# One ring of eight PSUM banks, and the scores of two batches next to each other on TensorE

## The chip, the core and the metric

One core of a Trainium2 chip runs the whole program. The metric is the time of one execution on the device in microseconds (us). PE is TensorE, which multiplies matrices; DVE is VectorE, ACT ScalarE, POOL GpSimd, and SP is SyncE, which issues most of the transfers (DMAs). PSUM is the memory into which TensorE writes: 8 banks of 2 KB per partition.

## What is computed

128 batches of 128 tokens with 512 features go through two graph layers, in float32:

```python
h = maximum(layernorm(x), 0)                        # layer 0
q, k, v = h @ Wq.T + bq, h @ Wk.T + bk, h @ Wv.T + bv   # 8 heads of 64
attn = softmax((q @ k.T) * SCALE * (adj + adj))     # per batch and head, 128 x 128
x = x + (attn @ v) @ Wo.T + bo
h = maximum(layernorm(x), 0)                        # layer 1
Wh = h @ W;  e = leaky_relu(Wh @ a[:512] + (Wh @ a[512:]).T)
att = softmax(where(adj > 0.5, e, -9e15), axis=1)
x = x + elu(att @ Wh)
```

## The kernel before

Work goes by pairs of batches (p = 0 to 63; batches a and b of a pair), and q, k and v are made for groups of two pairs. Everything is written as short named steps, and three lists of step names give the order: HEAD once, ORDER once per loop pass (57 passes), TAIL once. In HEAD and TAIL `step@p` names the pair (in TAIL counted from the end), in ORDER `step:lag` works on the pair that many passes back. A step that a pair does not have is skipped. The order on every engine and every queue is the order of these lists; nothing reorders it, and the tile pools only add the waits.

The steps that matter here, with the lines of their functions:

- `U1` to `U11` (L230 `product`): one of the 21 partial products of q, k, v, four matmuls 128x256 into a PSUM tile acc_a, acc_b or acc_c. `F` steps copy a finished tile out on ScalarE (L262, L267), `A` steps add one on VectorE (L271). Products of the same tile follow each other into the same bank.
- `sca`, `scb` (L302 `scores`): scores of batch a or b, eight matmuls that use 64 rows of the array each (one head each; heads on rows 0 to 63 and on rows 64 to 127 alternate). `ata`, `atb` (L315 `weigh`): VectorE multiplies the scores by the adjacency out of PSUM into the tile `at`. `mxa` (L323) takes the maxima, `exa0` to `exa3` (L327) the exponentials on ScalarE, `rca0/1` and `nma0` to `nma3` (L332, L336) normalise, `fla` (L343) flips 32x32 blocks on VectorE, `bla` and `pla` (L348, L352) send the blocks to DRAM and fetch them placed, one DMA and four, all on SyncE's queue.
- `pca`, `pcb` (L367 `context`): the context of a batch, eight matmuls of 64 columns each, into a tile pc; `pea` (L382) copies it out on ScalarE. `cs0` to `cs3` (L146 to L152) are sums on VectorE.
- `o0` to `o6` and `w0` to `w6` (L283 `product_rows`): the products with Wo and with W, two matmuls each into row_a or row_c; `od`, `wd` (L389, L471) add on VectorE and `zc` (L467) copies on ScalarE. `wd1` adds what `w1` made to what `zc0` copied. `gs0` to `gs3` are VectorE sums for W.
- `st0/1`, `pw`, `nm`, `h20/1`, `d..`, `pb`, `wm`, `g0/1`, `ge0/1`: layer 1, with `pw` on GpSimd and `pb`, `g` on TensorE.
- In the head, `lx`, `Lq`, `Lk`, ... load x and the weights on SyncE's queue; `Wq0` and the like (L132 `weight_sum`) are VectorE sums over a weight that has landed; `t0`, `t1` (L172) are row statistics, `pp` the power on GpSimd, `hn` (L178) normalises, `tp` (L186) transposes on TensorE, `ev` (L191) copies out on ScalarE.

PSUM is divided in two pools: `ps1`, six single banks that all other tiles take in turn, and `ps2`, one tile of two banks, only for scores. Scores of heads on rows 0 to 63 go into the first of the two banks, the others into the second.

In ORDER these steps stand as `sca:0 pca:1 pcb:1 scb:0` as far as TensorE is concerned: between them are steps of other engines only. So a loop pass has scores of batch a, two contexts of the pair before, and scores of batch b.

Of the kernel before, what the change touches and what calls it, by code (L numbers as in the profile page):

```python
# [13 lines left out]
P = 128  # L14
# [10 lines left out]
def kernel(  # L25
# [31 lines left out]
    ps1 = ctx.enter_context(tc.tile_pool(name="ps1", bufs=6, space=bass.MemoryType.PSUM))  # L57
    ps2 = ctx.enter_context(tc.tile_pool(name="ps2", bufs=1, space=bass.MemoryType.PSUM))
# [243 lines left out]
    def scores(b):  # L302
        p, i = divmod(b, 2)
        g, h = divmod(p, 2)
        qT, kT = qks[g, "q"][h], qks[g, "k"][h]
        cols = slice(i * S, (i + 1) * S)

        sc = ps2.tile([P, H, S], F32, name="sc", tag="ps2")
        for j in range(C):
            for s in range(2):  # L310
                r = slice(s * D, (s + 1) * D)
                nc.tensor.matmul(sc[:, s * C + j, :], qT[r, j, cols], kT[r, j, cols], start=True, stop=True)  # L312
        scs[b] = sc

    def weigh(b):  # L315
        p, i = divmod(b, 2)
        at = work.tile([P, H, S], F32, name="at")
        nc.vector.scalar_tensor_tensor(  # L318
            at, scs.pop(b), QSCALE, adjs[p][:, i : i + 1, :].to_broadcast([P, H, S]), op0=OP.mult, op1=OP.mult
        )  # L320
        ats[b] = at, small.tile([P, H], F32, name="nmx"), small.tile([P, H], F32, name="sums"), small.tile([P, H], F32, name="rs")
# [210 lines left out]
    def listed(text, mark):  # L532
# [3 lines left out]
        lx@0 t0@-5 Lu0@0 t1@-5 lt@0 Lq@0 Lk@0 pp@0 lx@1 hn0@0 hn1@0 tp0@0 Wq0@0 Lu1@0 t1@-4 t0@-4 tp1@0 pp@1 Wq2@0 hn0@1  # L536
        ev0@0 Lv@0 ev1@0 U3@-1 U5@-1 Wk0@0 U1@-2 lx@2 hn1@1 F1@-2 tp1@1 Lo@0 tp0@1 Wq1@0 la@-1 Lw@0 ev0@1 la@0 ev1@1
        t1@-3 t0@-3 U8@-2 U6@-2 F3@-1 pp@2 l0@-2 U2@-2 hs0@-3 F6@-2 l0@-1 hs1@-3 Wk1@0 U10@-2 Wv0@0 Lc@0 Wk2@0 Wk3@0
        hn0@2 hs2@-3 U7@-1 F7@-1 Wv1@0 A5@-1 hs3@-3 t0@-2 U3@-2 F10@-2 t1@-2 pp@3 A8@-2 hn1@3 tp0@2 U2@-1 U9@-1 hn0@3
        hn1@2 F3@-2 cu01@0 F2@-1 U4@-1 F9@-1 tp1@2 cu00@0 U8@-1 l0@0 ev0@2 ev1@2 A9@-1 U10@-1 tp0@3 Ww0@0 l0@1 t0@-1  # L540
        U11@-1 U5@-2 F4@-1 t1@-1 F10@-1 sca@0 F5@-2 tp1@3 ata@0 mxa@0 exa2@0 exa3@0 exa0@0 ccp@0 A2@-2 Wv2@0 ccd@0 U1@0
        ev0@3 t1@0 sh@0 ev1@3 rca1@0 U6@0 U7@-2 nma2@0 Wq3@0 t0@0 F6@0 hs0@-1 cu10@0 s0@-1 nma3@0 exa1@0 U1@-1 rca0@0
        lt@1 scb@0 hs1@-1 F7@-2 U3@1 nma0@0 nma1@0 A2@-1 fla@0 atb@0 U10@0 mxb@0 U6@-1 exb0@0 Wv3@0 U4@-2 t1@1 bla@0
        U2@0 exb2@0 A11@-1 exb1@0 rcb0@0 exb3@0 t0@1 nmb0@0 A5@-2 f0@0 rcb1@0 nmb1@0 nmb3@0 pla@0 s0@0 A6@-1 Wo0@0 U9@-2
        sup0@0 hs2@-1 nmb2@0 sca@1 Wo2@0 f0@1 flb@0 sua0@0 ata@1 blb@0 A9@-2 lT@1 F10@0 U8@0 F3@1 U2@1 A8@0 F1@0 mxa@1
        plb@0 la@1 cu11@0 hs3@-1 exa2@1 exa0@1 U3@0 F2@1 exa1@1 rca0@1 exa3@1 nma1@1 U5@1 U4@1 U7@1 A2@0 nma0@1 Wo1@0
        Ww2@0 rca1@1 scb@1 F4@1 Ww1@0 nma3@1 nma2@1 lT@0 F7@1 l0@2 pca@0 F3@0 A5@1 fla@1 pcb@0 pea@0 sup1@0 U9@1 atb@1
        mxb@1 peb@0 exb2@1 U8@1 U5@0 sua1@0 cs0@0 bla@1 s0@1 Ww3@0 hd0@0 pla@1 hd1@0 exb1@1 o0@0 f0@2 o1@0 F9@1 hd0@1
        hd1@1 exb3@1 exb0@1 U10@1 od0@0 F10@1 cs1@0 od1@0 rcb1@1 nmb3@1 U1@1 rcb0@1 nmb2@1 F5@0 o2@0 nmb1@1 A9@1 sca@2
        hs0@1 nmb0@1 A2@1 pca@1 U6@1 od2@0 Wo3@0 cs2@0 o4@0 flb@1 o3@0 ata@2 cs3@0 od4@0 U11@1 od4c@0 blb@1 o5@0 mxa@2  # L550
        o6@0 exa3@2 exa2@2 od5@0 hs2@1 exa0@2 exa1@2 U4@0 t1@2 rca1@2 nma3@2 hs1@1 A5@0 A6@1 od6@0 rca0@2 nma2@2 st0@0
        U7@0 pea@1 nma0@2 U1@2 A11@1 st1@0 o0@1 plb@1 nma1@2 F7@0 pcb@1 scb@2 sh@1 fla@2 pw@0 peb@1 atb@2 U2@2 o1@1
        mxb@2 F1@2 bla@2 nm@0 U3@2 h21@0 exb2@2 cs0@1 cs1@1 U4@2 U9@0 h20@0 A2@2 d11@0 od0@1 exb3@2 d00@0 od1@1 hs3@1
        d10@0 F3@2 o2@1 lT@2 d01@0 od2@1 exb0@2 rcb1@2 pb@0 exb1@2 U5@2 wm@0 rcb0@2 pr@0 F5@2 nmb1@2 cs2@1 U6@2 m1@0
        o4@1 e1@0 t0@2 lt@2 U7@2 nmb0@2 cs3@1 nmb3@2 A5@2 A9@0 pla@2 sw@0 F7@2 od4@1 o3@1 g0@0 nmb2@2 o5@1 ge0@0 od4c@1
    """
    ORDER = """
        F4:1 F6:1 flb:1 fb:4 U9:1 F9:1 g1:3 od5:2 ge1:3 o6:2 la:1 st0:2 s0:1 hd0:1 od6:2 U8:1 w0:3 st1:2 gs0:3 blb:1
        hd1:1 pw:2 w1:3 gs1:3 nm:2 U10:1 zc0:3 so:4 U1:0 gs2:3 h20:2 A9:1 A8:1 l0:0 wd1:3 w2:3 F10:1 gs3:3 h21:2 plb:1
        lx:1 hs0:1 zc2:3 lT:0 sca:0 pca:1 pcb:1 scb:0 w4:3 d00:2 d01:2 pea:1 A6:1 ata:0 mxa:0 peb:1 d10:2 w3:3 F1:0  # L560
        d11:2 cs0:1 t1:0 exa1:0 f0:0 exa3:0 pb:2 sh:1 A4:4 wm:2 zc4:3 exa2:0 exa0:0 pr:2 o0:1 o1:1 rca1:0 F8:0 nma3:0
        hs2:1 w5:3 hs1:1 wd4c:3 rca0:0 U2:0 nma1:0 cs2:1 cs1:1 nma2:0 m1:2 nma0:0 w6:3 od0:1 U11:1 od1:1 fla:0 U3:0
        zc5:3 atb:0 F2:0 mxb:0 F3:0 o2:1 e1:2 A10:16 cs3:1 wd6:3 U5:0 F5:0 sw:2 exb0:0 A2:0 U4:0 exb2:0 A3:28 exb3:0
        exb1:0 A5:0 A11:1 bla:0 o3:1 rcb1:0 od2:1 nmb2:0 U6:0 hs3:1 o4:1 lt:0 rcb0:0 nmb0:0 t0:0 nmb3:0 nmb1:0 pla:0
        U7:0 ez:3 F7:0 F11:-22 g0:2 fa:3 od4:1 A1:15 od4c:1 ge0:2 o5:1 A7:14
    """
    TAIL = """
        F4@-5 U9@-5 F9@-5 g1@-7 flb@-5 o6@-6 A6@-5 U10@-5 fb@-8 la@-5 ge1@-7 gs0@-7 F10@-5 so@-8 hd0@-5 od5@-6 blb@-5
        pca@-5 sca@-4 hd1@-5 pea@-5 la@-4 U5@-3 st0@-6 lx@-5 U8@-5 ata@-4 mxa@-4 exa0@-4 exa3@-4 exa1@-4 od6@-6 w0@-7
        hs0@-5 w1@-7 o0@-5 scb@-4 exa2@-4 st1@-6 pw@-6 U3@-3 gs2@-7 A9@-5 zc0@-7 nm@-6 rca0@-4 rca1@-4 hs1@-5 wd1@-7  # L570
        nma3@-4 nma0@-4 gs1@-7 nma2@-4 o1@-5 gs3@-7 plb@-5 sh@-5 nma1@-4 fla@-4 pcb@-5 atb@-4 U11@-5 od0@-5 U6@-4 F3@-3
        h21@-6 peb@-5 h20@-6 mxb@-4 exb0@-4 w2@-7 d10@-6 cs0@-5 exb3@-4 exb2@-4 zc2@-7 U7@-3 cs1@-5 A11@-5 d00@-6
        exb1@-4 od1@-5 w4@-7 F6@-4 d11@-6 o2@-5 pb@-6 rcb0@-4 od2@-5 rcb1@-4 wm@-6 nmb1@-4 d01@-6 nmb0@-4 sca@-3 w3@-7
        nmb2@-4 U10@-4 nmb3@-4 zc4@-7 w5@-7 cs2@-5 bla@-4 scb@-3 pr@-6 flb@-4 ata@-3 cs3@-5 hs2@-5 zc5@-7 pla@-4 m1@-6
        wd4c@-7 pca@-4 mxa@-3 w6@-7 F7@-3 o4@-5 od4@-5 wd6@-7 F10@-4 e1@-6 U2@-3 blb@-4 exa1@-3 exa0@-3 sw@-6 plb@-4
        fa@-7 exa2@-3 o5@-5 ez@-7 pea@-4 rca0@-3 g1@-6 nma0@-3 exa3@-3 o3@-5 la@-3 od5@-5 U9@-3 st0@-5 rca1@-3 od4c@-5
        g0@-6 o6@-5 ge1@-6 fb@-7 gs0@-6 o0@-4 A5@-3 nma2@-3 nma3@-3 pcb@-4 ge0@-6 nma1@-3 gs1@-6 w0@-6 o1@-4 fla@-3
        atb@-3 so@-7 lx@-4 mxb@-3 F9@-3 od6@-5 w1@-6 F2@-3 peb@-4 hs3@-5 cs0@-4 zc0@-6 wd1@-6 st1@-5 U8@-4 U10@-3 pw@-5
        bla@-3 exb3@-3 exb2@-3 exb1@-3 w2@-6 gs2@-6 gs3@-6 pla@-3 nm@-5 cs1@-4 exb0@-3 cs2@-4 rcb1@-3 la@-2 h21@-5
        rcb0@-3 zc2@-6 nmb3@-3 A8@-4 U8@-3 nmb2@-3 sh@-4 nmb0@-3 nmb1@-3 F10@-3 w4@-6 od0@-4 d11@-5 cs3@-4 od1@-4 zc4@-6  # L580
        d10@-5 U4@-3 F4@-3 U1@-3 sca@-2 flb@-3 w3@-6 h20@-5 ata@-2 o3@-4 mxa@-2 w5@-6 wd4c@-6 zc5@-6 d00@-5 exa0@-2
        o2@-4 od2@-4 w6@-6 o4@-4 A2@-3 d01@-5 wd6@-6 exa3@-2 od4@-4 lt@-4 exa1@-2 fa@-6 exa2@-2 pca@-3 ez@-6 U6@-3 pb@-5
        fb@-6 rca0@-2 blb@-3 o5@-4 od4c@-4 wm@-5 nma0@-2 rca1@-2 pr@-5 od5@-4 nma3@-2 A6@-3 o6@-4 plb@-3 nma1@-2 U1@-4
        U2@-4 nma2@-2 pcb@-3 m1@-5 scb@-2 st0@-4 pea@-3 od6@-4 st1@-4 fla@-2 e1@-5 A9@-3 so@-6 sw@-5 peb@-3 o0@-3 g1@-5
        g0@-5 U11@-3 ge1@-5 pw@-4 atb@-2 lx@-3 o1@-3 F1@-4 ge0@-5 cs0@-3 nm@-4 mxb@-2 cs2@-3 h21@-4 exb1@-2 gs0@-5 o3@-3
        w0@-5 sh@-3 lt@-3 w1@-5 exb0@-2 exb3@-2 h20@-4 gs1@-5 od0@-3 A11@-3 U3@-4 exb2@-2 A2@-4 rcb0@-2 d10@-4 cs1@-3
        zc0@-5 nmb0@-2 od1@-3 d00@-4 rcb1@-2 cs3@-3 o2@-3 d01@-4 wd1@-5 nmb1@-2 od2@-3 nmb2@-2 nmb3@-2 gs2@-5 sca@-1
# [46 lines left out]
    def steps(p):  # L634

        table = start_steps(p)
        for s, n in (("a", 2 * p), ("b", 2 * p + 1)):
            table |= {
                "sc" + s: lambda n=n: scores(n),
                "at" + s: lambda n=n: weigh(n),  # L640
                "mx" + s: lambda n=n: maxima(n),
                "fl" + s: lambda n=n: flip_blocks(n),
                "bl" + s: lambda n=n: send_blocks(n),
# [121 lines left out]
```

## Time and profile before

| what | value |
| --- | --- |
| median of 3 runs | 2380.54 us (2380.22 to 2381.16) |
| the profiled execution, its own time | 2378.95 us |
| its span, first to last instruction | 2377.1 us |
| granted TensorE clock | 1.000 |
| ScalarE busy | 1457.4 us (61%) |
| DMA | 306.10 MB, mean 129 GB/s |

The page of the profile gives busy time per engine, and the chain of work that ended last, followed back from the last instruction to what released each step. Groups of instructions are listed by line, engine and operation with the tiles that they write and read: `at<-sc,adj` is the tile `at` made from `sc` and `adj`; x128 is the count, then busy us and mean ns of one, then the idle time of the engine just before. A float32 matmul of the program is two records in the trace (1024 score matmuls are 2048 records). The modelled durations of matmuls overlap, so lengths on TensorE are taken between starts.

### The profile page before, as it was taken

Reading aid. Unit: us, or ns where it says so; the run is one execution under the profiler, and the core shown is the slowest. Engines: PE = TensorE matmul, PEld = TensorE weight load, DVE = VectorE, ACT = ScalarE, POOL = GpSimd, SP = SyncE. Lnnn points to the kernel's source line nnn. Section 1 sums busy time; section 2 is a strip of 40 time slices with the busy share of each in tenths; the row PEclk is TensorE's granted clock in tenths of the full one; section 3 lists DMA queues with packets and bytes.
Section 4 is the critical chain, followed back from the end, with each engine's and each line's share of the span. In section 5 each row is a group of like instructions: output and inputs, shape, how many; then the busy total and the mean of one; then the engine's idle time right before and its main releaser. Section 6 shows DMA issues by size and latency. Waiting matters only on the chain.

```text
span 2377.1 us, 40536 instructions
## 1 busy us (share of the span) xinstructions
PE 2355.3 (99%) x14264; PEld 2062.0 (87%) x14264; DVE 1988.5 (84%) x3909; ACT 1457.4 (61%) x4811; POOL 265.7 (11%) x323
## 2 busy tenths in 40 slices
PE   8999999999999999999999999999999999999998
PEld 7888888888888888888888888888888888888886
DVE  6878888888888888888888888888888888888787
ACT  3656566665666665656656666556656566665764
POOL 1011110111101101111111011111110111111000
PEclk9999999999999999999999999999999999999999
DMA  4444544554534545445455455453454544544332
GB/s 173 123 129 116 138 130 121 137 133 129 142 111 126 154 121 138 111 118 158 116 138 133 118 137 137 128 145 107 125 160 116 138 111 123 153 120 125 108 113 93
DMA packets 255275, 306.10 MB, mean 129 GB/s; under 512 B 21856, under 2 KB 181600, under 8 KB 254432
## 3 DMA queue, kind: packets, MB, share of 16 engines
q1 hardware_dynamic: 251568, 303.37, 46.5%
q8 instruction: 113, 1.85, 0.3%
q0 software_dynamic: 1920, 0.13, 0.2%
q14 instruction: 90, 0.74, 0.1%
q10 hardware_dynamic: 1584, 0.01, 0.0%
HBM read 202.64 MB, written 100.79 MB: 128 GB/s over the span
## 4 chain that ended last, share of the span: by engine, by line
PE 99%; DMA 1%; DVE 0%; ACT 0%; issue 0%; DVEq 0%
PE acc_a L250 28%; PE row_a L291 24%; PE acc_c L250 14%; PE row_c L291 9%; PE acc_b L250 7%; PE sc L312 6%; PE pc L375 5%; PE pg L453 5%; PE pb L421 1%; DMA wk<-in_wkT 0%; PE pm L494 0%; DMA bq<-in_bq 0%; PE pt L189 0%; DVE junk L412 0%; DVE x L479 0%
## 5 line engine op out<-in xcount | busy, mean ns | idle before, releaser
L330 ACT ACTIVATE at<-at,nmx 128x128 f32<-128x128 f32 x1024 | 397.0, 393 | 23.0 <-DVE nmx L325 22.0
L291 PE MATMUL row_a<-w,gT 128*128 128x256 f32 x1280 | 325.4, 385 | 2.8 <-DVE z L471 1.7
L339 ACT ACTIVATE at<-at,rs 128x128 f32<-128x128 f32 x1024 | 317.8, 390 | 15.3 <-DVE rs L334 15.2
L291 PE MATMUL row_a<-wo,cxT 128*128 128x256 f32 x1280 | 319.5, 380 | 0.4 <-DVE cxT L148 0.4
L164 POOL TENSOR_SCALAR mv<-mv 128x2 f32<-128x2 f32 x128 | 78.9, 616 | 2057.8 <-DVE mv L161 1999.3
L467 ACT COPY z<-row_a 128x256 f32<-128x256 f32 x256 | 92.6, 362 | 298.5 <-PE row_a L291 297.9
L291 PEld LDWEIGHTS row_a<-w,gT 128*128 128x128 f32 x1280 | 237.3, 190 | 42.0 <-DVE z L471 2.5
L291 PEld LDWEIGHTS row_a<-wo,cxT 128*128 128x128 f32 x1280 | 233.8, 190 | 28.1 <-DVE cxT L148 0.6
L318 DVE SCALAR_TENSOR_TENSOR at<-sc,adj 128x1024 f32<-128x1024 f32 x128 | 156.7, 1225 | 92.2 <-PE sc L312 89.7
L267 ACT ACTIVATE kT<-acc_a,bk 128x256 f32<-128x256 f32 x256 | 107.3, 470 | 156.7 <-PE acc_a L250 155.1
L330 ACT ACTIVATION_READ_ACCUMULATOR at<-at,nmx 128x1 f32 x1024 | 195.5, 191 | 0.0
L346 DVE STREAM_TRANSPOSE tr<-at 128x1024 f32<-128x1024 f32 x128 | 158.7, 1240 | 33.0 <-ACT at L339 29.8
L160 DVE BATCH_NORM_STATS2 st<-x 128x6 f32<-128x512 f32 x256 | 175.3, 685 | 10.9 <-DMA x<-in_x 6.7
L389 DVE TENSOR_TENSOR x<-row_a,x 128x256 f32<-128x256 f32 x320 | 132.8, 415 | 50.6 <-PE row_a L291 48.3
L262 ACT COPY v<-acc_a 128x512 f32<-128x512 f32 x128 | 74.7, 584 | 150.0 <-PE acc_a L250 150.0
L325 DVE TENSOR_REDUCE nmx<-at 128x8 f32<-128x1024 f32 x128 | 156.1, 1220 | 4.2
L382 ACT COPY cxT<-pc 128x512 f32<-128x512 f32 x128 | 74.9, 585 | 127.3 <-PE pc L375 127.1
L312 PEld LDWEIGHTS sc<-kT,qT 64*128 64x128 f32 x2048 | 124.2, 187 | 32.4 <-issue 32.0
L312 PE MATMUL sc<-kT,qT 64*128 64x128 f32 x2048 | 148.7, 285 | 0.0
L165 POOL TENSOR_TENSOR mv<-mv,mhalf 128x2 f32<-128x2 f32 x128 | 140.2, 1095 | 10.7
L453 PEld LDWEIGHTS pg<-w,h 128*128 128x128 f32 x1024 | 133.7, 192 | 6.6 <-ACT z L467 0.2
L453 PE MATMUL pg<-w,h 128*128 128x128 f32 x1024 | 134.4, 275 | 0.0
(126 smaller groups left out, 4987.0 us busy)
## 6 DMA issues: line engine op xcount, KB each, us to landing
blocks<-tr SPq DMA_DIRECT2D x128, 512.0 KB, 5.1
aT<-blocks SPq DMA_DIRECT2D x512, 128.0 KB, 3.0
x<-in_x SPq DMA_DIRECT2D x123, 512.0 KB, 5.4
out<-x SPq DMA_DIRECT2D x64, 512.0 KB, 5.5
hA<-in_xT SPq DMA_DIRECT2D x120, 256.0 KB, 4.4
mr<-rows SPq DMA_DIRECT2D x60, 256.0 KB, 5.1
adjT<-in_adjT SPq DMA_DIRECT2D x64, 128.0 KB, 3.7
adj<-in_adj SPq DMA_DIRECT2D x64, 128.0 KB, 2.9
```

The lines of the kernel that those rows point to most:

```text
L160: nc.vector.bn_stats(st, src[:, i, :])
L165: nc.gpsimd.tensor_tensor(mv[:, :, 1], mv[:, :, 1], mhalf.to_broadcast([P, 2]), OP.pow)
L250: nc.tensor.matmul(acc[:, m, :], lhsT, rhs, start=fresh and m == 0 and c == 0, stop=c == 1, skip_group_check=True)
L291: nc.tensor.matmul(acc, left[:, la, c, :], w[:, wb, c, :], start=n in (0, 3) and c == 0, stop=c == 1, skip_group_check=True)
L312: nc.tensor.matmul(sc[:, s * C + j, :], qT[r, j, cols], kT[r, j, cols], start=True, stop=True)
L318: nc.vector.scalar_tensor_tensor(at, scs.pop(b), QSCALE, adjs[p][:, i : i + 1, :].to_broadcast([P, H, S]), op0=OP.mult, op1=OP.mult)
L325: nc.vector.tensor_reduce(nmx, at, AX.X, OP.max, negate=True)
L330: nc.scalar.activation(at[:, j, :], at[:, j, :], AF.Exp, bias=nmx[:, j : j + 1], accum_out=sums[:, j : j + 1])
L339: nc.scalar.activation(at[:, j, :], at[:, j, :], AF.Copy, scale=rs[:, j : j + 1])
L346: nc.vector.transpose(trs[b], at.rearrange("p h (j k) -> p j h k", k=Q))
L389: nc.vector.tensor_tensor(d, row_acc(p, "o", bank), d, OP.add)
L453: nc.tensor.matmul(pg[:, c, :], h1s[p][0][:, i, c * P : (c + 1) * P], wts[p][:, i, :], start=True, stop=True)
```

## The change

The two PSUM pools become one ring of eight single banks. A batch's scores take two tiles of one bank each from that ring, one for each half of the array's rows. The weigh becomes two steps of four heads each, `ata0` and `ata1`, so 256 instructions of 128x512 in place of 128 of 128x1024; the tile `at` and the small tiles are made at the first of the two. All three lists are new.

```diff
-    ps1 = ctx.enter_context(tc.tile_pool(name="ps1", bufs=6, space=bass.MemoryType.PSUM))
-    ps2 = ctx.enter_context(tc.tile_pool(name="ps2", bufs=1, space=bass.MemoryType.PSUM))
+    ps1 = ctx.enter_context(tc.tile_pool(name="ps1", bufs=8, space=bass.MemoryType.PSUM))
...
-        sc = ps2.tile([P, H, S], F32, name="sc", tag="ps2")
+        sc = [ps1.tile([P, C, S], F32, name="sc", tag="ps1") for _ in range(2)]
...
-                nc.tensor.matmul(sc[:, s * C + j, :], qT[r, j, cols], kT[r, j, cols], start=True, stop=True)
+                nc.tensor.matmul(sc[s][:, j, :], qT[r, j, cols], kT[r, j, cols], start=True, stop=True)
...
-    def weigh(b):
+    def weigh(b, k):
         p, i = divmod(b, 2)
-        at = work.tile([P, H, S], F32, name="at")
+        if b not in ats:
+            ats[b] = work.tile([P, H, S], F32, name="at"), *(small.tile([P, H], F32, name=n) for n in ("nmx", "sums", "rs"))
         nc.vector.scalar_tensor_tensor(
-            at, scs.pop(b), QSCALE, adjs[p][:, i : i + 1, :].to_broadcast([P, H, S]), op0=OP.mult, op1=OP.mult
+            ats[b][0][:, k * C : (k + 1) * C, :], scs[b][k], QSCALE, adjs[p][:, i : i + 1, :].to_broadcast([P, C, S]),
+            op0=OP.mult, op1=OP.mult,
         )
```

In the new ORDER the steps around the scores stand as follows (before: `w1 ... zc0 ... lT sca pca pcb scb ... ata mxa`):

```diff
+        U1:0 A9:1 F10:1 pw:2 so:4 hs2:1 A1:8 ge1:3 F8:-4 gs0:3 w0:3 nm:2 w1:3 zc0:3 sca:0 F11:1 h20:2 wd1:3 gs2:3 scb:0
+        h21:2 A4:8 ata0:0 ata1:0 pca:1 lx:1 hs1:1 pcb:1 mxa:0 pea:1 F1:0 U11:1 gs1:3 lT:0 exa1:0 A6:1 d00:2 U2:0 exa3:0
```

So TensorE has `w0 w1`, the scores of a, the scores of b, both contexts, and then `U11` or `U2`. The new HEAD begins:

```diff
-        lx@0 t0@-5 Lu0@0 t1@-5 lt@0 Lq@0 Lk@0 pp@0 lx@1 hn0@0 hn1@0 tp0@0 Wq0@0 Lu1@0 t1@-4 t0@-4 tp1@0 pp@1 Wq2@0 hn0@1
+        lx@0 Lq@0 t0@-5 lx@1 Lo@0 Lk@0 Wq0@0 t1@-5 pp@0 t1@-4 lx@2 Lc@0 t0@-4 hn0@0 pp@1 Lv@0 hn1@0 tp0@0 Lw@0 tp1@0
```

The new TAIL ends, as the old one does, with the layer 1 steps of the last pairs; in it the scores stand alone more often than in ORDER.

## The prediction

> **What bounds the kernel now.** I read the page's busy shares first, then the chain that ended last, then TensorE's timeline over one pair in mid-run, then the waits.
>
> ```profile
> PE 2355.3 (99%) x14264; PEld 2062.0 (87%) x14264; DVE 1988.5 (84%) x3909; ACT 1457.4 (61%) x4811; POOL 265.7 (11%) x323
> PE 99%; DMA 1%; DVE 0%; ACT 0%; issue 0%; DVEq 0%
> ```
>
> TensorE is busy 99% of the span and carries 99% of the chain that ended last. So an edit counts only where it shortens TensorE's stream or makes TensorE wait. VectorE is idle (2377.1 - 1988.5) / 64 = 6.1 us per pair, ScalarE 14 us. But busy is not dense, so I went to the starts:
>
> ```profile
> 1015.97 1.89 PE L250 MATMUL acc_c<-hS,wq 128*128 128x256 f32 x8
> 1017.70 1.03 PE L291 MATMUL row_a<-w,gT 128*128 128x256 f32 x4
> 1018.65 1.16 PE L312 MATMUL sc<-kT,qT 64*128 64x128 f32 x16
> 1019.74 1.97 PE L375 MATMUL pc<-aT,v 128*64 128x128 f32 x32
> 1021.64 1.16 PE L312 MATMUL sc<-kT,qT 64*128 64x128 f32 x16
> 1022.73 1.13 PE L291 MATMUL row_a<-w,gT 128*128 128x256 f32 x4
> 1023.70 1.03 PE L291 MATMUL row_c<-w,gT 128*128 128x256 f32 x4
> ...
> 2277.16 1.09 PE L375 MATMUL pc<-aT,v 128*64 128x128 f32 x16
> 2278.19 1.99 PE L250 MATMUL acc_c<-hA,wq 128*128 128x256 f32 x8
> ```
>
> Columns are start, duration, engine, work. Subtract starts. Eight full-array matmuls take 1.73 us (0.216 each), so four should take 0.86; the four ahead of the scores take 0.95, and the four behind take 0.97. The scores of a batch (16 records) take 1.09. Two contexts in a row (32 records) take 1.90 and one (16) takes 1.03, so a second context adds only 0.87, and the first pays 0.15 extra. The shapes column says why: full-array work is 128*128, scores use 64 rows, contexts 64 columns, and each change of kind costs. From the single starts: inside scores a pair of records repeats every 0.112 us, but the first pair takes 0.213 and the exit 0.201 in place of 0.105. A stretch of scores thus pays 0.197 once, a stretch of contexts 0.151, a stretch of full-array work 0.198 (0.094 at its end, 0.104 on its first matmul).
>
> ```profile
> DVE at L318 <- PE sc L312: 89.7, 63, 3.7
> PEld acc_a L250 <- ACT v L262: 6.0, 28, 0.2
> ```
>
> (Engine and line, whom it waited for, us, times, longest.) The first shows VectorE standing ready for the scores, 1.4 us a time. The second is the only steady wait of TensorE: it lengthens its start by 0.08 us at 27 places, 2.2 us in all, every second pair, where only four matmuls (0.86) stand between two products into one bank, while the copy between needs 0.32 + 0.58.
>
> **The change part by part.** *Stretches on TensorE.* I counted stretches in the instruction order of both programs. Scores: 128 before, 66 after (62 of two batches, 4 of one). Contexts: 70 and 68. Full-array: 77 and 74. Saved: 62 x 0.197 + 2 x 0.151 + 3 x 0.198 = 12.2 + 0.3 + 0.6 = **13.1 us**. The number of matmuls is the same. All of it is on the path: TensorE ends the chain.
>
> *The steady wait.* In the new order at least 1.7 us of other products stand between two products into one bank wherever ScalarE must copy in between, and the longest copy path (0.32 + two activations of 0.36 and 0.47) is 1.2. The wait goes: **-2.2 us**. Bounds: -2.2 to 0.
>
> *The new wait: contexts take the banks of the scores.* Bank numbers in the built program show that in every steady pair the first context writes into the bank that the first half-scores of batch a held, and the second into the other half's. So the context waits for the first new weigh (ata0). Walk it, zero at the first score matmul: the last write to that bank starts at 0.78 (seven pairs); from a last score matmul to VectorE's start the trace has 0.319, so ata0 starts at 1.10; it is 128x512 out of PSUM, and the row nearest is the add out of a bank, 0.687 us below; end 1.79; from VectorE's end to TensorE's start the tail shows 0.055: 1.84. Without a wait the context would start at 0.213 + 14 x 0.112 + 0.208 = 1.99. Slack **0.14 us**. VectorE must also be free at 1.10: ahead of ata0 are wd1 (0.415) and gs2 (0.418), 0.33 apart; wd1 waits for ScalarE's zc0 (0.362), which waits for w1's last matmul, 0.31 ahead of zero: zc0 runs 0.01 to 0.37, wd1 from 0.42, gs2 from 0.75, VectorE is free at 1.08. It fits with almost nothing to spare; what else queues behind (ata1, the maxima, then mask and dots) is as late as ata0. I take **0**; bounds 0 to 0.15 us x 57 loop passes = 8.6 us. A gain is excluded: no context waited for a bank before.
>
> Here a rule speaks against the change. The Trainium skill, "TensorEngine Tiling (Array Packing)", PSUM Bottleneck, says that packed matmuls speed up TensorE but not the emptying of PSUM, which may become the limit. By it, four weighs of 0.687 = 2.75 us must empty what TensorE fills in 1.99, and the 0.76 missing would cost 57 x 0.76 = 43 us. By the rows, the contexts need only two of the four banks, one after the other, and the next user of batch b's banks comes 8 us later or more in the bank list. I go by the rows.
>
> *The weigh in halves.*
>
> ```profile
> L318 DVE SCALAR_TENSOR_TENSOR at<-sc,adj 128x1024 f32<-128x1024 f32 x128 | 156.7, 1225 | 92.2 <-PE sc L312 89.7
> L271 DVE TENSOR_TENSOR v<-acc_c,v 128x512 f32<-128x512 f32 x64 | 43.9, 687 | 52.1 <-PE acc_c L250 52.0
> ```
>
> Two of 687 for one of 1225: +149 ns x 128 = 19 us of busy VectorE, 0.3 us per pair. The skill's "Perfetto Trace Analysis", Optimizing Scalar/DVE Operations, prices an extra instruction on PSUM at about 125 ns, 16 us by it. Either lies in VectorE's 6.1 us idle per pair: **0** on the path. Without that cover it would be the 19 us.
>
> *Head.*
>
> ```profile
> 10.60 0.69 DVE L135 TENSOR_TENSOR wq<-wq 128x512 f32<-128x512 f32 x1 [2.94 <-DMA wq<-in_wqT]
> 13.16 3.53 PE L250 MATMUL acc_a<-hA,wk 128*128 128x256 f32 x8 [3.94 <-DMA wk<-in_wkT]
> ```
>
> Today the first product waits for wk. Anew, SyncE sends wq right behind the first x, so wq should land between 7.5 (full rate) and 9.6 (today's 10.6 less the 0.38 MB now behind it). But VectorE now has a sum on wq (Wq0) ahead of the second row statistics, so these start only then: + 0.6 (Wq0) + 0.9 (statistics) + 4.35 (today's time from the end of these statistics, 5.52, to the second copied half, 9.87: power, normalise, transposes, copy) + 0.55 (VectorE does the second pair's statistics in between) = first product at 13.9 to 16.0, less 0.44 for four more transposes done by then. Against 13.16: +0.3 to +2.4; I take **+1.2**. Bo, wo and wv are needed later than they land.
>
> *Tail.* Before, waits of TensorE in the last 50 us add up to 6.3 us, and 7.6 us follow its last matmul's start. The closing steps stand in nearly the same order. From the last scores to the last context there are 22.0 us of TensorE work (21.7 before), but laid on the rows' durations the last weigh comes some 4 us after its scores, behind the flip of the batch ahead (1.8 before), so transposed blocks should land late by 0 to 3 us. I take **+1.0**; bounds -1 to +3.
>
> *Sum*, against the profiled execution (2378.95, span 2377.1): -13.1 - 2.2 + 0 + 0 + 1.2 + 1.0 = -13.1, that is 2365.9. The median lies 1.6 above the profiled one, so **2367.4**.
>
> **The rivals.**
> *A small bank wait* (ata0 late by 0.05 to 0.15 beyond its slack): +3 to +9, 2370 to 2376. For it: VectorE is free only 0.02 ahead. Against: 0.14 of slack after it. 0.14.
> *A large bank wait, slower.* Place: the first context of each pair. If VectorE still has one 0.69 instruction more ahead of ata0 (the accumulator add A9, a statistics), ata0 is 0.69 late, TensorE waits 0.55 x 57 = 31 us: 2399. It beats the saving from a wait of 13.1 / 57 = 0.23, a lateness of 0.37. Against: VectorE waited 1.4 us for scores in 63 cases. 0.04.
> *The change doesn't do what it says*: the 0.197 is paid per batch (new bank, new operands) and not per stretch; then -13.1 becomes about 0: 2380. Against: 32 contexts in a row show no step at the batch's edge (0.103 as inside). 0.04.
> *Head and tail gain*: full-rate landing and a shorter drain, 2357 to 2363. 0.08.
>
> **How the numbers follow.** Forecast, 2363 to 2371: 0.70. The range 2362 to 2376 takes in the small bank wait and the bounds of head and tail. A measurement tells 0.2% (4.8 us) from no change: faster is below 2375.8. Forecast, small wait and the last rival give 0.91; same 0.05; slower 0.04.
>
> **What would show it.** Score stretches of 32 records taking 1.99 us, with no 0.2 step in the middle; contexts 0.201 behind their last matmul: later means the bank wait, and then a wait of context on weigh appears in the list. The ScalarE wait gone. Weigh 128x512 near 690 ns, x256, VectorE near 2008 us. First product at 14 to 16. Wrong would be: a pair's period in mid-run not shorter by 0.20 us, or VectorE reaching ata0 late.

## The result, and the profile after

The changed kernel takes 2367.41 us (median of 4 runs, 2366.41 to 2367.53); the kernel before took 2380.38 in the same session. The ratio is 0.9945, with a 95% interval of 0.9928 to 0.9962. The forecast was 2367.4. The profiled execution took 2367.53 us with a span of 2365.8, against 2378.95 and 2377.1: 11.3 us less span. That the total is right does not yet say that its terms are.

First the page of the changed kernel: busy times, the chain that ended last by engine, and the group of the weigh (count, then busy us and mean ns of one, then idle time ahead).

```profile
PE 2340.5 (99%) x14264; PEld 2060.4 (87%) x14264; DVE 2006.5 (85%) x4037; ACT 1437.9 (61%) x4811; POOL 222.7 (9%) x323
...
PE 98%; DVE 1%; issue 0%; DMA 0%; ACT 0%; POOL 0%; SPq 0%; DVEq 0%; ACTq 0%; POOLq 0%
...
L318 DVE SCALAR_TENSOR_TENSOR at<-sc,adj 128x512 f32<-128x512 f32 x256 | 169.9, 685 | 4.5 <-PE sc L311 2.0
```

TensorE executes as many records as before in 15 us less busy time and still carries 98% of the chain. VectorE is 18 us busier and at 85%. It stood 92.2 us idle ahead of weighs before and stands 4.5 now: it no longer waits for the scores, it arrives late itself. That is the point where the change comes closest to losing what it gains.

Next the timeline of TensorE over one pass in mid-run. The columns are start, duration, engine and work, as before.

```profile
1010.90 1.89 PE L290 MATMUL row_a<-w,gT 128*128 128x256 f32 x8
1012.72 2.06 PE L311 MATMUL sc<-kT,qT 64*128 64x128 f32 x32
1014.70 1.97 PE L375 MATMUL pc<-aT,v 128*64 128x128 f32 x32
1016.60 1.99 PE L249 MATMUL acc_a<-hS,wq 128*128 128x256 f32 x8
1018.43 1.89 PE L249 MATMUL acc_a<-hA,wk 128*128 128x256 f32 x8
```

Subtract starts: 32 score records take 1.98 us, against 2 x 1.09 = 2.18 in two stretches; 32 contexts take 1.90, as before. In the single starts all 32 score records go in steps of 0.112 us a pair from the second pair on, with nothing at the batch's edge. The period of a pair, averaged over 40 pairs of mid-run (from one product with the second layer's mask, line 421, to the one 40 pairs later), is 36.311 us, against 36.542 before: 0.231 less.

The last view is the list of waits of TensorE's weight loads (who waited for whom: us, times, longest).

```profile
PEld pc L375 <- DMA aT<-blocks: 2.0, 1, 2.0
...
PEld pc L375 <- DVE at L318: 0.8, 2, 0.4
```

The row of 28 waits for ScalarE's copy is gone. A new row stands in the list, a context that waits for a weigh, but only twice in the run. The first row is in the closing steps.

### The profile page after: what moved, and what is told of

It is laid out like the page before. It is cut to its first block, busy times and chain, and to the rows that moved or that the text cites. A ratio compares the mean times of both kernels' runs of the same rounds, so it can differ in the third digit from the quotient of the medians.

```text
span 2365.8 us, 40912 instructions
## 1 busy us (share of the span) xinstructions
PE 2340.5 (99%) x14264; PEld 2060.4 (87%) x14264; DVE 2006.5 (85%) x4037; ACT 1437.9 (61%) x4811; POOL 222.7 (9%) x323
## 4 chain that ended last, share of the span: by engine, by line
PE 98%; DVE 1%; issue 0%; DMA 0%; ACT 0%; POOL 0%; SPq 0%; DVEq 0%; ACTq 0%; POOLq 0%
PE acc_a L249 28%; PE row_a L290 23%; PE acc_c L249 14%; PE row_c L290 9%; PE acc_b L249 7%; PE sc L311 5%; PE pc L375 5%; PE pg L453 5%; PE pb L421 1%; DVE junk L412 0%; DMA wq<-in_wqT 0%; PE pt L188 0%; DVE st L159 0%; POOL mv L164 0%; PE pm L494 0%
## 5 line engine op out<-in xcount | busy, mean ns | idle before, releaser
L339 ACT ACTIVATE at<-at,rs 128x128 f32<-128x128 f32 x1024 | 323.6, 394 | 4.0 <-DVE rs L334 3.9
L290 PE MATMUL row_a<-w,gT 128*128 128x256 f32 x1280 | 319.5, 380 | 1.7 <-ACT z L467 1.4
L290 PEld LDWEIGHTS row_a<-w,gT 128*128 128x128 f32 x1280 | 242.1, 190 | 37.1 <-ACT z L467 2.6
L163 POOL TENSOR_SCALAR mv<-mv 128x2 f32<-128x2 f32 x128 | 30.5, 239 | 2089.2 <-DVE mv L160 2054.8
L266 ACT ACTIVATE qT<-acc_a,bq 128x256 f32<-128x256 f32 x256 | 106.4, 469 | 164.1 <-PE acc_a L249 164.1
L318 DVE SCALAR_TENSOR_TENSOR at<-sc,adj 128x512 f32<-128x512 f32 x256 | 169.9, 685 | 4.5 <-PE sc L311 2.0
L164 POOL TENSOR_TENSOR mv<-mv,mhalf 128x2 f32<-128x2 f32 x128 | 145.5, 1137 | 10.6
L290 PE MATMUL row_c<-w,gT 128*128 128x256 f32 x512 | 131.6, 379 | 1.0 <-DVE z L471 1.0
L311 PE MATMUL sc<-kT,qT 64*128 64x128 f32 x2048 | 132.4, 279 | 0.0
```

The lines of the kernel that those rows point to most:

```text
L164: nc.gpsimd.tensor_tensor(mv[:, :, 1], mv[:, :, 1], mhalf.to_broadcast([P, 2]), OP.pow)
L266: nc.scalar.activation(dst(t, f)[:, m, :], a[:, m, :], AF.Identity, bias=bias[:, j : j + 1])
L290: nc.tensor.matmul(acc, left[:, la, c, :], w[:, wb, c, :], start=n in (0, 3) and c == 0, stop=c == 1, skip_group_check=True)
L311: nc.tensor.matmul(sc[s][:, j, :], qT[r, j, cols], kT[r, j, cols], start=True, stop=True)
L318: nc.vector.scalar_tensor_tensor(ats[b][0][:, k * C : (k + 1) * C, :], scs[b][k], QSCALE, adjs[p][:, i : i + 1, :].to_broadcast([P, C, S]) ...
L339: nc.scalar.activation(at[:, j, :], at[:, j, :], AF.Copy, scale=rs[:, j : j + 1])
```

## The experiments

Every kernel was timed beside the kernel before on the same chip. The changed kernel itself was timed in its own session only; the kernel before has medians of 2379.1 to 2379.4 in the later ones, 1.0 to 1.3 us lower, so differences of about 1 us between the changed kernel and a run are not shown by the medians. The first group undoes or isolates parts; the second tests what the trace after had shown of slack and head. None leaves out any part of the computation.

| run | median us | ratio to before, 95% interval | period of a pair, us |
| --- | --- | --- | --- |
| the kernel before (all sessions) | 2379.1 to 2380.4 | | 36.542 |
| the changed kernel | 2367.41 | 0.9945 (0.9928 to 0.9962) | 36.311 |
| apart | 2379.93 | 1.0004 (0.9996 to 1.0012) | 36.553 |
| ring | 2379.34 | 1.0001 (0.9993 to 1.0010) | 36.542 |
| joined_before | 2458.46 | 1.0334 (1.0320 to 1.0348) | 37.940 |
| late | 2386.03 | 1.0030 (1.0018 to 1.0041) | 36.628 |
| freed | 2367.59 | 0.9952 (0.9939 to 0.9964) | 36.304 |
| contexts_apart | 2406.86 | 1.0117 (1.0104 to 1.0131) | 37.001 |
| head | 2368.13 | 0.9953 (0.9940 to 0.9967) | 36.324 |
| both | 2367.39 | 0.9952 (0.9940 to 0.9965) | 36.304 |
| head_product | 2366.70 | 0.9947 (0.9935 to 0.9959) | 36.337 |
| product_first | 2369.97 | 0.9960 (0.9946 to 0.9973) | 36.318 |
| best | 2366.34 | 0.9946 (0.9933 to 0.9958) | 36.304 |

A period is the mean of 40 pairs in one profiled execution, so one wait of 1 us among them adds 0.025. Those of apart, head, head_product and product_first contain such waits (2.03, 0.50, 1.04 and 0.26 us in all), each before the second of two contexts; the changed kernel and the last three of these also have one context among them that is late by the weigh (0.26).

### Is it the stretch that pays? The run apart

```diff
-  ... sca:0 F11:1 h20:2 wd1:3 gs2:3 scb:0 h21:2 A4:8 ata0:0 ata1:0 pca:1 lx:1 hs1:1 pcb:1 mxa:0 ...
+  ... sca:0 F11:1 h20:2 wd1:3 gs2:3 h21:2 A4:8 ata0:0 ata1:0 pca:1 lx:1 hs1:1 pcb:1 scb:0 mxa:0 ...
```

> The changed kernel with the second batch's scores moved behind both contexts: scores, two contexts, scores. Ring, halves and all else stay; nothing is left out of the computation. Theory (a stretch of scores pays its 0.197 us once, whatever stands in it): 57 passes of the loop get one score stretch more and one full-array stretch fewer or the same, 57 x 0.19 = +11 us over the changed kernel, 2378.5 (2376 to 2381), which undoes nearly all of the gain. Rival (the price is paid per batch, and the gain came from the other parts): 2367 to 2369. In the trace the theory wants score stretches of 16 records, near 1.09 us each, where one of 32 stood.

Measured: 2379.93 us, level with the kernel before. Its TensorE timeline:

```profile
1055.14 1.16 PE L311 MATMUL sc<-kT,qT 64*128 64x128 f32 x16
1056.23 1.97 PE L375 MATMUL pc<-aT,v 128*64 128x128 f32 x32
1058.13 1.16 PE L311 MATMUL sc<-kT,qT 64*128 64x128 f32 x16
```

Two stretches of 1.09 us stand where one of 1.98 stood: 57 x 0.198 = 11.3 us. Another 2.0 us come from two passes, at 582 and 1495 us, in which the second context starts late; that was not expected. In both, the last of the four DMAs that place its transposed block takes 6.8 and 6.6 us to land (the median of all is 3.3), and the context starts 0.1 and 0.4 us after the landing. Less these two waits the period is 36.503, which is 0.198 above that of freed, a run below without late contexts. With ring, halves and all other orders in place, moving this one step gives the gain back: 11.3 us of it by the stretch, the rest by these waits. The rival, a price per batch, falls.

### Does the storage alone bring anything? The run ring

The kernel before with `bufs=8` in one pool, two single-bank score tiles, and each `ata` of its lists replaced by `ata0 ata1`; its order is otherwise untouched.

> The kernel before, with only its storage changed: eight single banks in one ring, scores of a batch in two of them, weigh in halves, the order of all steps as before (each whole weigh replaced by its two halves). Theory (ring and halves enable the new order and bring nothing by themselves): the same as before, 2380 +- 2, VectorE 19 us busier, TensorE's stretches unchanged; of the 2.2 us in waits for ScalarE's copies, some or none may go. Rival (the ring itself, which frees banks earlier, brings a good part of the gain): 2368 to 2374. Second rival (VectorE's extra 19 us count): 2388 to 2399.

Measured: 2379.34 us, and a pair's period equal to that of the kernel before to the fourth decimal (36.5421). Its groups and its waits:

```profile
L318 DVE SCALAR_TENSOR_TENSOR at<-sc,adj 128x512 f32<-128x512 f32 x256 | 164.9, 686 | 91.2 <-PE sc L311 88.7
```

```profile
PEld acc_a L249 <- ACT v L261: 6.0, 28, 0.2
```

Both rivals fall: the ring brings nothing, and VectorE's extra work costs nothing. The second row shows more: the steady wait for ScalarE's copy stays, with the same numbers, in a ring of eight. So the banks alone do not take it away; in the changed kernel it is the new order that does. The first row corrects a size. A half has a mean of 686 ns, but two that follow each other overlap, so the group is busy 164.9 us, 8 more than the 156.7 of the whole weighs, not 19.

### Does the joined order need the ring? The run joined_before

```diff
-  ... lT:0 sca:0 pca:1 pcb:1 scb:0 w4:3 ...
+  ... lT:0 sca:0 scb:0 pca:1 pcb:1 w4:3 ...
```

> The kernel before, with the two batches' scores put together in the steady order and nothing else changed: six single banks and one tile of two banks for scores. Nothing is left out. Theory (the joined order needs the ring): the second batch's scores must wait until the first batch's weigh has read the only score tile; from the last score matmul of the first batch that is 0.32 + 1.23 + 0.06 us against 0.1 without a wait, so 1.5 us and more a pair where other VectorE work stands ahead of the weigh, less 0.2 for the stretch: 57 x 1.3 and more, 2450 to 2490. Rival (the order alone brings the gain, the ring is idle): 2367 to 2370.

Measured: 2458.46 us, within the expected range. TensorE's timeline, with the idle time and its releaser in brackets:

```profile
1052.81 1.16 PE L312 MATMUL sc<-kT,qT 64*128 64x128 f32 x16
1055.30 1.16 PE L312 MATMUL sc<-kT,qT 64*128 64x128 f32 x16 [1.33 <-DVE at L318]
1056.39 1.97 PE L375 MATMUL pc<-aT,v 128*64 128x128 f32 x32
```

The second stretch starts 2.49 us after the first, not 1.09: 1.40 more in each of 57 passes, 80 us. So neither part stands alone. The order saves the stretch, the ring makes the order possible. Whether the ring would do with whole weighs, or another division of the eight banks as well, was not tested.

### How much slack has the context? The runs late and freed

The walk of the prediction gave 0.14 us between the first weigh's end and the context that writes into its bank. The timeline of the changed kernel around one pair of scores (VectorE and ScalarE among TensorE):

```profile
1012.72 2.06 PE L311 MATMUL sc<-kT,qT 64*128 64x128 f32 x32
1012.87 0.37 ACT L467 COPY z<-row_a 128x256 f32<-128x256 f32 x1 [2.18 <-issue]
...
1013.27 0.42 DVE L471 TENSOR_TENSOR z<-row_a,z 128x256 f32<-128x256 f32 x1 [1.74 <-ACT z L467]
1013.62 0.41 DVE L149 TENSOR_TENSOR gT<-gT 128x256 f32<-128x256 f32 x1
1013.95 1.28 DVE L318 SCALAR_TENSOR_TENSOR at<-sc,adj 128x512 f32<-128x512 f32 x2
...
1014.70 1.97 PE L375 MATMUL pc<-aT,v 128*64 128x128 f32 x32
```

From the first score: zc0 at 0.15, wd1 at 0.55, gs2 at 0.90, the first weigh at 1.23; its half ends at 1.91 (in the single records, the median of 58 stretches), and 0.055 later is 1.97, when the context would have started anyway at 1.985. The slack is 0.017 us. The run late puts 0.33 us of VectorE work (`gs1`) ahead of the first weigh; the run freed takes 0.42 away (`gs2` goes behind the second).

```diff
 late
-  ... h21:2 A4:8 ata0:0 ata1:0 pca:1 ...
+  ... h21:2 A4:8 gs1:3 ata0:0 ata1:0 pca:1 ...
 freed
-  ... wd1:3 gs2:3 scb:0 h21:2 A4:8 ata0:0 ata1:0 pca:1 ...
+  ... wd1:3 scb:0 h21:2 A4:8 ata0:0 ata1:0 gs2:3 pca:1 ...
```

> The changed kernel with one VectorE step (a logarithm's row operation of the second layer, 0.33 us) moved ahead of the first weigh; nothing is left out. It tells how much slack the contexts have before they wait for the banks that the first scores held. Theory read off the trace after (slack 0.02 us): each joined stretch makes TensorE wait 0.33 - 0.02 = 0.31 us, 57 x 0.31 = +18 us, 2385 (2380 to 2388). By the prediction's slack of 0.14: 57 x 0.19 = +11 us, 2378. Rival (contexts do not wait for that bank at all): 2367. In the trace the theory wants contexts 0.3 us late behind the last score matmul, with the weigh named in the waits.

> The changed kernel with one VectorE step (gs2, a 0.42-us subtraction of the second layer) moved from ahead of the two first weighs to behind them; nothing is left out. VectorE then is free about 0.33 us earlier, so the first weigh starts when the bank allows it. Theory (the last write into the first bank is in the eighth pair of score records, 0.88 us after the first): the first weigh starts 1.19 after the first score, ends 1.88, slack 0.05 us; the two late places (0.26 each) go; the time is that of the changed kernel, 2367 less 0.5. By the prediction's walk (last write in the seventh pair, 0.78) it would start at 1.10 and leave 0.14. Rival (something behind gs2 becomes late, the row products that read it): above 2370.

Measured: late takes 2386.03 us, slower than the kernel before. Its waits:

```profile
PEld pc L375 <- DVE at L318: 25.5, 57, 0.7
```

All 57 stretches now have the wait. The first weigh starts 0.335 later, the context 0.317, and 0.335 - 0.017 is 0.318; 57 x 0.317 = 18.1 us, of the 18.6 by which its median lies above that of the changed kernel in the other session. By the slack of the prediction it would have been 0.195 a pass, 11 us. So a third of a microsecond on an engine that is 15% idle turns the gain into a loss.

Freed takes 2367.59, as the changed kernel. Its waits show VectorE standing ready again:

```profile
DVE at L318 <- PE sc L311: 13.8, 57, 1.1
```

The first weigh now starts at 1.193, at the earliest moment that any of the traces shows, and not at 1.10. The two late contexts are gone, and a pair's period is 0.0065 shorter, which is one of the two among 40 pairs (0.26 / 40); together they are 0.5 us, too little for the whole time to show.

### Do contexts pay too? The run contexts_apart

```diff
-  ... zc0:3 sca:0 F11:1 h20:2 wd1:3 gs2:3 scb:0 h21:2 A4:8 ata0:0 ata1:0 pca:1 lx:1 hs1:1 pcb:1 ...
+  ... zc0:3 pca:1 sca:0 F11:1 h20:2 wd1:3 gs2:3 scb:0 h21:2 A4:8 ata0:0 ata1:0 lx:1 hs1:1 pcb:1 ...
```

> The changed kernel with the first batch's context moved ahead of the joined scores, the second left behind them: the scores stay one stretch, the contexts become two; nothing is left out. Theory (a stretch of contexts pays 0.151 us once): 57 x 0.151 = +8.6 us, 2376 (2374 to 2378). Rival (the price of a change of kind lies with the scores alone): 2367. Second rival (the moved context takes a bank that is not free yet): a wait of context in the list and more than 2380. Score stretches should keep their 1.985 us.

Measured: 2406.86 us, the second rival. Its timeline:

```profile
1064.87 1.09 PE L375 MATMUL pc<-aT,v 128*64 128x128 f32 x16
...
1065.89 2.60 PE L311 MATMUL sc<-kT,qT 64*128 64x128 f32 x32
1066.71 0.57 ACT L382 COPY cxT<-pc 128x512 f32<-128x512 f32 x1
...
1067.33 0.96 PEld L311 LDWEIGHTS sc<-kT,qT 64*128 64x128 f32 x14 [0.25 <-ACT cxT L382]
```

The scores stop in their middle until ScalarE has copied the moved context: the shift in the ring makes the second batch's scores need its bank at once. The stretch takes 2.533 in place of 1.985. The two prices add up: 57 x 0.151 for the extra context stretch (the two contexts take 1.024 each, 2.048, against 1.898) is 8.6, 57 x 0.548 is 31.2, together 39.8; measured against the changed kernel 39.5. The stretch price of the contexts stands, read from the records, and a ring of eight does not serve every order.

### What holds the head? The runs head, product_first, head_product, both, best

On VectorE, head puts the first pair's normalising ahead of the sum on wq and of the second pair's statistics. On TensorE, product_first puts the first product (`U6@-2`) ahead of the second pair's transposes (`tp1@1`). The run head_product does both, the run both is head with freed, the run best is head_product with freed. The edit of head_product:

```diff
-  lx@0 Lq@0 t0@-5 lx@1 Lo@0 Lk@0 Wq0@0 t1@-5 pp@0 t1@-4 lx@2 Lc@0 t0@-4 hn0@0 pp@1 Lv@0 hn1@0 tp0@0 Lw@0 tp1@0
-  Lu0@0 ev0@0 hn1@1 ev1@0 hn0@1 tp1@1 Wq1@0 U6@-2 Wq2@0 ...
+  lx@0 Lq@0 t0@-5 lx@1 Lo@0 Lk@0 t1@-5 pp@0 lx@2 Lc@0 hn0@0 Lv@0 hn1@0 Wq0@0 t1@-4 t0@-4 pp@1 tp0@0 Lw@0 tp1@0
+  Lu0@0 ev0@0 ev1@0 U6@-2 hn1@1 hn0@1 tp1@1 Wq1@0 Wq2@0 ...
```

> The changed kernel with the opening order mended: the sum on wq and the second pair's row statistics no longer stand ahead of the first pair's normalising on VectorE; nothing is left out. Theory (the head's loss is this queue): TensorE's first transposes start near 7.3 us as in the kernel before, not at 11.6, and its first product near 10 to 11, not 14.2; up to 3.5 us can be gained, 2364 to 2366. Rival (a later transfer holds the next products, so that the first merely starts earlier): TensorE stops again before 20 us, 2367.

> The changed kernel with TensorE's order alone mended: the first product ahead of the second pair's transposes, VectorE's opening order as it was; nothing is left out. Theory (both hold the head): the first product still needs the first pair's second copied half, which comes at 14.2 because VectorE's queue is late, so it starts at 14.2 as before, and little is gained: 2366.5 to 2367.5.

> The changed kernel with the mended opening order of the run head, and the first product moved ahead of the second pair's transposes on TensorE; nothing is left out. Theory (the head is held twice: by VectorE's queue, and by TensorE's own order, which puts four transposes that need the second pair's x ahead of the first product): the first product starts at 10 to 11 us instead of 14.2, is done when the second pair's x is normalised near 13.5, and 3 to 3.5 us are gained: 2364 to 2365. Rival (something later, wk or a weight sum, holds the following products): a new stop of TensorE before 25 us and 2367.

> Both edits at once (the subtraction behind the first weighs, and the mended opening order). Theory: the two add up, 0.5 and 1 to 3.5 us below the changed kernel, 2363 to 2366. Rival: as for the two alone, 2367.

> The changed kernel with the subtraction behind the first weighs (as in the run freed) and both opening orders mended (as in the run head_product). Theory: the gains add, 2363.5 to 2365, below both kernels of the study. Rival: as in head_product, 2367.

Measured: the theory of head failed. Its timeline:

```profile
7.84 1.97 PE L188 MATMUL pt<-ident,hn 128*128 128x128 f32 x8 [7.84 <-DVE hn L181]
13.58 1.12 PE L188 MATMUL pt<-ident,hn 128*128 128x128 f32 x4 [3.78 <-DVE hn L181]
14.49 3.20 PE L249 MATMUL acc_a<-hA,wq 128*128 128x256 f32 x8
```

The first transposes come 3.7 us earlier, but four transposes of the second pair stand ahead of the first product, and their x, its statistics and the power on GpSimd take until 13.6. TensorE's own order holds the head as much as VectorE's queue does. Only with both mended does the product move, as the timeline of head_product shows:

```profile
8.03 1.97 PE L188 MATMUL pt<-ident,hn 128*128 128x128 f32 x8 [8.03 <-DVE hn L181]
10.68 3.78 PE L249 MATMUL acc_a<-hA,wq 128*128 128x256 f32 x8 [0.69 <-ACT hA L191]
14.26 1.91 PE L188 MATMUL pt<-ident,hn 128*128 128x128 f32 x8
```

The product starts 3.5 us earlier, at 10.68, and there is no new stop before 25 us. Not all of this reaches the end. TensorE runs at half rate at first (last section): behind the product's start that lasts until 16.82 here and costs 3.1 us, against 1.5 in the changed kernel, where it lasts until 17.19; and the four transposes that now come behind the product take 0.4. Of the 3.5 us, 1.5 are left at the first record of line 421 (127.15 against 128.69 us). Another 1.0 is lost at 579 us, where a second context waits for a block that takes 7.3 us to land (median 3.5). In the profiled execution of best half rate ends at 15.21, no context of the loop is late, and the span is 2362.7, 3.1 us below that of the changed kernel.

The medians show less: 2366.70 for head_product, and 2366.34 (2364.47 to 2368.39) for best. That is below both kernels of the study, but by about 1 us and with intervals that overlap that of the changed kernel, so best is shown faster than the kernel before only. Head, head_product, both and best came out 1.3 to 2.1 us above the upper end of what was expected of them. Product_first, expected at 2367, took 2369.97: VectorE's queue held its product until 14.97, 0.8 later than in the changed kernel; the four transposes that others do while they wait now came behind it (0.4); and half rate lasted until 19.85, which cost 0.9 more.

## Why the prediction was right, step by step

*The stretch on TensorE* (-13.1): right, and shown. In the loop, 0.198 from the stretch and 28 x 0.08 / 57 = 0.039 from the wait make 0.237 a pair; the period fell by 0.231, and the one late context among its 40 pairs (0.26 / 40 = 0.0065) accounts for what lacks: in freed, without it, the period fell by 0.238. Apart takes it away again, contexts_apart shows the contexts' share.

*The steady wait* (-2.2): gone, as forecast. Ring shows that the storage alone does not remove it.

*The new bank wait* (0): the value was right, the working was not, and nearly cost the forecast. Two terms of the walk were mis-sized. First, "the last write to that bank starts at 0.78 (seven pairs)": each pair of records has one of either half, so the first bank is complete only with the eighth pair, at 0.88. The earliest weigh of all traces starts at 1.19, and freed, where VectorE is ready, shows just that. Second, "zc0 runs 0.01 to 0.37": ScalarE starts 0.15 after the first score, so VectorE is free at 1.23, not 1.08. The slack of 0.14 was 0.017. For the small bank wait the prediction gave a chance of 0.14; it came within 0.02 us of happening, and did so in two passes. Late shows the price beyond the slack to be one to one, and that a loss begins at about a quarter of a microsecond (0.231 + 0.017), not at the 0.37 that was forecast.

The rule on PSUM (43 us) did not bind, for the reason given: only the weigh of the first bank, and after it that of the second, stand between the scores and the contexts.

*The weigh in halves* (0 on the path): right. The busy time forecast, 2008 us, came within 2 of the 2006.5 measured, partly by chance: the weighs grew by 13.2 us, not 19 (8 where they always follow each other, in ring), and other rows of VectorE by 5. That is 103 and 64 ns for each added instruction; the 125 ns of the Trainium skill ("Perfetto Trace Analysis", Optimizing Scalar/DVE Operations) would have been 16 us.

*Head* (+1.2): the first product started at 14.21, inside the forecast 13.9 to 16.0, 1.05 later than before. Idle or slow time of TensorE up to 30 us went from 13.9 to 14.4, so the term was 0.5. One execution each tells little. In apart, late, freed and contexts_apart, whose opening is the same, wq lands later (its sum starts at 8.54 to 9.61, not at 7.87), the product starts at 14.83 to 15.85, and idle or slow time is 13.8 to 15.5. In ring and joined_before, with the opening of the kernel before, the product starts at 12.65 and 12.84, and that time is 14.7 and 14.5. By the means of these eight the term is 0.4, less than the spread within one opening. The cause named, the sum on wq in VectorE's queue, was half of it. The views of the changed kernel's head:

```profile
7.87 0.69 DVE L134 TENSOR_TENSOR wq<-wq 128x512 f32<-128x512 f32 x1 [3.15 <-DMA wq<-in_wqT]
...
11.55 2.82 PE L188 MATMUL pt<-ident,hn 128*128 128x128 f32 x12 [11.55 <-DVE hn L181]
...
14.21 3.45 PE L249 MATMUL acc_a<-hA,wq 128*128 128x256 f32 x8
```

Twelve transposes stand ahead of the product, not eight; what these four wait for was priced only as work already done.

*Tail* (+1.0): mis-sized. Waits of TensorE after 2300 us went from 6.4 to 8.7, and 0.15 more follow its last matmul: +2.4. Most of it, 1.7, is the context at 2328 that waits for its transposed block (it is in the first row of the waits above): the last weigh starts 5 us after its scores, behind the flip of the batch ahead, which is the place that the prediction named. No experiment was made on it; it is read from the trace.

*The sum.* Forecast -15.3 + 1.2 + 1.0 = -13.1; by the trace -11.3 of span. Taking off head (+0.5) and tail (+2.4) leaves -14.2 for stretches and waits. The counted stretches and the steady wait at their measured prices, less the two late contexts (0.5), would be about -14.9, so some 0.7 us is not located. The stretches and waits thus gave 1 us less than forecast, the tail took 1.4 more and the head 0.7 less; the median of the runs lies 13.0 below that of before, since the profiled execution of the changed kernel (2367.53) was at the upper end of its runs and that of before (2378.95) below all of its others. That the forecast hits the median to a tenth is luck of this size.

## What to carry over

On an engine that sets the end, count how often the kind of work changes, not only how much work there is: here one change more per pass costs 0.20 us. Before joining two stretches, walk the banks from the last write of each to the first reader and on to the next writer, record by record; a slack of hundredths of a microsecond is invisible in busy shares and is lost one to one. And before an opening is mended on one engine's queue, read the order of the engine that waits: what stands ahead of the wanted instruction in its own queue must be ready too.

## What was not expected of the hardware

The first matmuls run at half rate. Between starts a product's matmul takes 0.43 us until about 17 us of the changed kernel's span, and 0.216 from there on: compare the product at 14.21 (3.45 us) with those in mid-run (1.89 us). The view of the granted clock gives 1.00 for these stretches, but that is not measured there: the trace's record of this clock begins only at 17.19 us, where the steps change, and time without a record counts as full (so it does in the 1.000 given for the kernel before). In the thirteen profiled executions the record begins after 3.1 us (contexts_apart) to 6.1 (both, head_product) of unbroken work on TensorE. How long the clock then stays full tells more: 2341.54 us in both, 2344.96 in the changed kernel and five others, 2355.20 in ring, 2358.61 in apart and in the kernel before. All thirteen lengths differ by whole multiples of 3.413 us, although the kernels differ by other amounts: the clock changes on a grid of its own.

The Trainium skill, "TensorE: Matmul & The Clock Gate", What's actually happening, tells of a clock that starts at half and is released after sustained work, by a window of that length that doesn't start with the kernel. Under What you observe it puts the change near 4 us, give or take 0.5, and the traces here spread more widely, over 3.0 us, nearly one step of the grid. Each us at half rate costs half a us, so this spread is 1.5 us from one execution to another. That is as large as what the edits of the head could bring. In the profiled executions it can be taken off, as was done above; whether it is what moves the medians, whose other executions left no trace, is not shown.
